# Graph attention on one core: three more tiles of the output pairs turned by VectorE, and another share of attention work beside the units ahead of the output stage

## The chip, the cores and the metric

The kernel runs on one core of a Trainium2 chip. The metric is the device time of one execution in microseconds (us). Before the change three runs gave 636.95, 638.43 and 638.96 us, so the median is 638.43 us.

The engines are named as in the profile: PE is TensorE (matrix products and transposes by a matrix product), PEld its weight loads, DVE is VectorE, ACT is ScalarE, POOL is GpSimd (here it mostly starts indirect gathers and scatters), SP is SyncE (here it only starts DMAs). "PEq", "ACTq", "SPq" are the sequencers of these engines.

## The reference

One layer of graph attention on 2708 nodes of 1024 features, in fp32, with a residual. `adj` is a random 0/1 matrix with some four ones in a row.

```python
h = relu(layernorm(x))                      # x: 2708 x 1024
q = h @ W_q.T + b_q;  k = h @ W_k.T + b_k;  v = h @ W_v.T + b_v
z = (q @ k.T) / sqrt(1024) * adj
z = where(z == 0, -10000, z)
out = x + relu(softmax(z, axis=1) @ v)
```

## The kernel before

Only the scores of existing edges are needed. The kernel sorts the nodes by their number of edges and cuts them into 21 full tiles of 128 nodes and a rest. Since z = h M h^T with M = scale * W_q^T W_k (plus a bias), PE forms M once, then q' = h M for the tiles; a score is the dot product of a row of q' with a gathered row of h. The weighted sum of rows of h is taken before W_v: u = sum(weight * h[neighbour]), and then out = relu(u W_v^T + b_v) + x.

**Units on PE.** PE multiplies two tiles at a time by Strassen's scheme (Winograd's form): a pair is a 256 x 1024 matrix in four blocks (a11 and a12 from the first tile, a21 and a22 from the second), and takes seven products instead of eight, each 8 records of 128x128 by 128x512 in the trace, about 3.43 us. The units are numbered: 0 to 9 are "q" pairs (tiles (0,1) to (18,19)), 10 to 19 are output pairs in the order (6,5), (4,3), (2,0), (20,7), (17,13), (18,12), (19,11), (15,10), (14,1), (16,9), and tile 8 alone stands behind them. So "the sixth output pair" is unit 15 with tiles 18 and 12, and the seventh is unit 16 with tiles 19 and 11. The operands are sums and differences of blocks: s1 = a22 + a21, s3 = a11 - a21, s2 = s1 - a11, s4 = a12 - s2 (L722, L742), and four sums and differences of W_v's blocks (T0 to T3, L1270, each 128x2048 elements), which VectorE forms in units 9 and 10, before the first output pair. After a unit's last product c22 (`q` L1092) and c12 (L1095) add PSUM banks on VectorE; PE's next product into the same bank waits for that.

**Turning a tile.** The operand must lie transposed. There are two ways.
- By PE: u is stored to `u_dram` by SP (L951) and loaded by SP as one DMA of 512 KB (L1212), or kept in SBUF (`held`) when its unit comes soon. PE transposes it in eight products of 128x128 (L415) into PSUM banks `pt`, ScalarE copies a11, a12 and a22 to SBUF (L718), and VectorE takes a21 from PSUM directly when it forms s1 and s3.
- "Faced": ScalarE copies u into another order of columns (v, L945) and stores it from its own queue (L947); SP loads it as four DMAs of 128 KB, each of 32 partitions (L700), so that four blocks of the 128x128 transpose already stand in their places; VectorE transposes 32x32 blocks within them (L705), one instruction of 128x512 for each of a11, a12, a22 and a21 (which stands in the buffer of s3). PE and the copies L718 are not needed.

**Attention as a stream.** The attention work is one generator, `attention`, of steps on VectorE. A score step is one multiply-and-accumulate with a gathered row tile (`junk` L863), a sum step adds one weighted row tile (`u` L923); a step is planned at 1.3 us. Between them stand small instructions for the softmax (L906 to L911), ScalarE's exponential (`w` L872) and ScalarE's first term of u (L912, or L889 for the tile numbered 21). Every tile gathered needs one of 11 buffers (g0 to g10, later also pieces of M's space), which its last reader frees.

**What sets the order.** After the fourth unit the order on VectorE is the one in which the program is written. After each product of a unit `advance(share)` lets the stream go on until its planned cost has reached `share` us, so a larger share puts more score and sum steps ahead of what the unit itself needs (blocks, c12, c22, differences). The orders of PE, ScalarE, POOL and SP come from a scheduler, so they shift when VectorE's program shifts. When tile t's sum is finished at `now` = [unit, place], where places 0 to 6 count the products, the condition at L940 decides whether it is faced. The share (L1238) goes down by 2.3/7 us a product for each faced tile of the next unit.

Lines for the steps below: L415, L718, L722, L742, L705 (turning), L700, L947, L951, L1212 (DMAs of u), L863, L923 (stream), L872, L889, L912 (ScalarE within the stream), L1100 (ScalarE's copy of c21), L760 (biases into PSUM banks), L1223 and L1224 (PE's sum of all rows of h and its copy), L1270 (W_v's sums), L1092 (c22), L1011 (products).

Of the kernel before, what the change touches and what calls it, by code (L numbers as in the profile page):

```python
# [65 lines left out]
def tile_preln_masked_attention(  # L66
# [144 lines left out]
    def row_tile(name):  # L211
        return work.tile([P, D], FT, tag="row", name=name, bufs=ROWS)
# [626 lines left out]
    def fill():  # L839
        while wanted and free:  # L840
            t, s = wanted.pop(0)
            g = free.pop(0)
            if s == K[t]:
                half = slice(HOSTS.index(t) * HP, (HOSTS.index(t) + 1) * HP)
                nc.gpsimd.dma_start(g[:HP], v_dram[half, :])
            else:
                with tc.issue_after(first_q[0].ins) if first_q else nullcontext():
                    gathered.append(gather(g, h_dram[:, :], t, s, P, skip=True))
            g_of[t].append(g)

    def chained(step):

        with tc.issue_after(chain[-1].ins):
            chain.append(step())
# [64 lines left out]
    def sums(t):  # L919
        u, coef, m = us.pop(t)  # L920
        for s in range(0 if t in EMPTY else 1, K[t]):
            fill()
            chained(lambda: nc.vector.scalar_tensor_tensor(  # L923
                u, g_of[t][s], coef[:, s:s + 1], u, op0=ALU.mult, op1=ALU.add))
            free.append(g_of[t][s])
            yield 1.3
        fill()
        if t in HOSTS:
            chained(lambda: nc.vector.scalar_tensor_tensor(
                u[:HP], g_of[t][K[t]][:HP], m[:HP, 3:4], u[:HP], op0=ALU.mult, op1=ALU.add))  # L930
            free.append(g_of[t][K[t]])
            yield 1.3
            fill()
        g_of.pop(t)
        if t == SECOND:
            nc.sync.dma_start(v_dram, u)
            whole_second.append(True)
            return
        unit = next((n for n, pair in enumerate(units) if pair[0] == "o" and t in pair[1:]), len(units))
        if now < [unit - 2, 2] and unit <= len(q_pairs) + 4 or unit >= len(units) - 1:  # L940
            faced_tiles.add(t)
        print("done", t, "at", now, "unit", unit, t in faced_tiles)
        if t in faced_tiles:
            v = row_tile(f"v_{t}")
            nc.scalar.copy(v.rearrange("p (a c r) -> p c a r", a=QUADS, r=QP),  # L945
                           u.rearrange("p (c a r) -> p c a r", a=QUADS, r=QP))
            nc.scalar.dma_start(u_dram[t * P:(t + 1) * P, :], v)  # L947
        elif near(t):
            held[t] = u
        else:  # L950
            nc.sync.dma_start(u_dram[t * P:(t + 1) * P, :], u)  # L951
        done.add(t)
# [7 lines left out]
    def attention(order):  # L960
        for t in order[:2]:
            ask(t)
        free.extend(slots)

        fetch(order[0])
        fill()
        yield 0.0
        marked(0, EARLY)
        yield 0.0
        after = order[1:] + [None, None]  # L970
        yield from scores(order[0], after[0])
        for i, t in enumerate(order):
            nxt = after[i]
            ahead = nxt is not None and K[t] + K[nxt] <= HIGH + 1
            part = scores(nxt, after[i + 1]) if nxt is not None else iter(())
            if ahead:

                for _ in range(min(2, K[nxt] - 1)):
                    yield next(part, 0.0)
            weights(t)  # L980
            yield 0.6
            if ahead:
                yield from part
            yield from sums(t)
            yield from part
# [8 lines left out]
    spent, now = [0.0], [0, 0]  # L994

    def near(t):

        return t == alone or any(t in unit[1:] for unit in units[:now[0] + 3] if unit[0] == "o")
# [193 lines left out]
    q_pairs = [(t, t + 1) for t in range(0, BARE, 2)]  # L1192
    o_pairs = [(order[i], order[i + 1]) for i in range(0, FULL - 1, 2)]
    alone = order[-1]
    units = [("q",) + p for p in q_pairs] + [("o",) + p for p in o_pairs]
# [20 lines left out]
    last_q = len(q_pairs) - 1  # L1216
# [13 lines left out]
    for n, unit in enumerate(units):  # L1230
# [4 lines left out]
            ordered.enter_context(tc.manual_schedule(engines={mybir.EngineType.DVE}))  # L1235
            nc.sync.dma_start(bp_dram, bp_sb[0:1, :])
        turn = n in (0, FIRST - 1)
        share = (20.9 if n < len(units) - 5 else 21.5) / 7  # L1238
        nxt = units[n + 1] if n + 1 < len(units) else None
        if nxt is not None and nxt[0] == "o":  # L1240
            share -= 2.3 / 7 * len(set(nxt[1:]) & faced_tiles)
# [321 lines left out]
```

## Time and profile before

| What | us |
|---|---|
| median of three runs | 638.43 |
| the profiled execution | 638.0 |
| its span | 636.3 |
| granted TensorE clock (share of full) | 0.995 |
| PE busy in the span | 624.6 |
| DVE busy | 525.7 |
| ACT busy | 283.5 |
| POOL busy | 361.8 |

All the times in what follows are counted from the start of the span. The stages are: M's formation until about 105, units 0 to 9 until about 365 (with the next unit's first two products drawn ahead), units 10 to 19 until about 610, the single tile until 627.3, and then the last additions and scatters. An instruction's row in the timeline has its start, its length, its engine, line, operation and tile; consecutive instructions of VectorE overlap by some 0.05 to 0.1 us, so that two in a row take a little less than the sum of their lengths. In brackets stand the idle time ahead of it and what ended this.

### The profile page before, as it was taken

Reading aid. Unit: us, or ns where it says so; the run is one execution under the profiler, and the core shown is the slowest. Engines: PE = TensorE matmul, PEld = TensorE weight load, DVE = VectorE, ACT = ScalarE, POOL = GpSimd, SP = SyncE. Lnnn points to the kernel's source line nnn. Section 1 sums busy time; section 2 is a strip of 40 time slices with the busy share of each in tenths; the row PEclk is TensorE's granted clock in tenths of the full one; section 3 lists DMA queues with packets and bytes.
Section 4 is the critical chain, followed back from the end, with each engine's and each line's share of the span. In section 5 each row is a group of like instructions: output and inputs, shape, how many; then the busy total and the mean of one; then the engine's idle time right before and its main releaser. Section 6 shows DMA issues by size and latency. Waiting matters only on the chain.

```text
span 636.3 us, 6139 instructions
## 1 busy us (share of the span) xinstructions
PE 624.6 (98%) x1627; PEld 315.5 (50%) x1627; DVE 525.7 (83%) x1021; ACT 283.5 (45%) x421; POOL 361.8 (57%) x383
## 2 busy tenths in 40 slices
PE   9999999999999999999999999999999999999994
PEld 5777766444444544444444434444444444444441
DVE  5999889897995755997889999999999989898341
ACT  3539975859667533424341243443343333422300
POOL 2649960975868277563742563576566777632431
PEclk9999999999999999999999999999999999999997
DMA  8998897598696439986699998999999999893761
GB/s 339 407 372 310 334 351 298 199 342 328 246 382 221 170 113 334 326 299 196 194 289 323 297 412 216 311 318 324 351 378 321 334 299 295 242 289 95 210 217 40
DMA packets 62352, 180.11 MB, mean 283 GB/s; under 512 B 10039, under 2 KB 17031, under 8 KB 61672
## 3 DMA queue, kind: packets, MB, share of 16 engines
q0 software_dynamic: 25136, 78.41, 39.4%
q1 hardware_dynamic: 31242, 80.19, 35.8%
q10 hardware_dynamic: 5934, 21.06, 8.5%
q8 instruction: 15, 0.25, 0.2%
q14 instruction: 25, 0.20, 0.1%
HBM read 147.23 MB, written 42.31 MB: 298 GB/s over the span
## 4 chain that ended last, share of the span: by engine, by line
PE 85%; DVE 6%; issue 4%; DMA 3%; SPq 1%; POOL 0%; ACT 0%; POOLq 0%; DVEq 0%; ACTq 0%
PE ps L1011 38%; PE psy L1011 28%; PE ps_y L476 6%; PE ps_x L476 4%; PE ps_z L476 4%; PE pt L415 3%; DVE u L923 2%; DMA g<-h_dram,tab 1%; DMA or<-u_dram 1%; DVE junk L863 1%; DVE s L722 1%; DVE wlow L1270 1%; PE ps_y L511 1%; SPq L700 1%; DVE q L1092 0%
## 5 line engine op out<-in xcount | busy, mean ns | idle before, releaser
L610 POOL DMA_INDIRECT g<-h_dram,tab x94 | 121.4, 1291 | 84.4 <-DVE u L923 31.1
L1011 PE MATMUL ps<-M,a 128*128 128x512 f32 x320 | 144.0, 593 | 0.0
L1011 PE MATMUL psy<-wlow,s 128*128 128x512 f32 x320 | 143.9, 592 | 0.0
L863 DVE SCALAR_TENSOR_TENSOR junk<-g,pq 128x1024 uint8<-128x1024 f32 x93 | 113.7, 1222 | 14.0 <-DMA g<-h_dram,tab 10.9
L1011 PEld LDWEIGHTS ps<-M,a 128*128 128x128 f32 x320 | 59.8, 190 | 70.8 <-issue 70.6
L1011 PEld LDWEIGHTS psy<-wlow,s 128*128 128x128 f32 x320 | 59.7, 190 | 70.2 <-issue 69.4
L923 DVE SCALAR_TENSOR_TENSOR u<-g,coef,u 128x1024 f32<-128x1024 f32 x69 | 88.4, 1281 | 6.9 <-ACT u L912 5.8
L389 DVE FIND_INDEX8 at<-ones,adj 128x8 uint32<-128x685 f32 (+1 forms) x88 | 74.5, 865 | 0.0
L1011 PE MATMUL psy<-wlow,a 128*128 128x512 f32 x160 | 72.0, 593 | 1.4 <-DVE q L1092 1.4
L1011 PE MATMUL ps<-M,s 128*128 128x512 f32 x160 | 72.1, 592 | 0.0
L1011 PE MATMUL ps<-wlow,s 128*128 128x512 f32 x160 | 72.0, 593 | 0.1
L368 ACT ACTIVATE sized<-adj 128x2708 uint8<-128x2708 f32 (+1 forms) x22 | 54.3, 2468 | 7.5 <-DMA adj<-in_adj_dram 6.2
L298 POOL TENSOR_TENSOR hsum<-hsum,x 128x256 f32<-128x256 f32 (+1 forms) x56 | 38.7, 729 | 25.6 <-DVE wlow L444 21.2
L1110 POOL DMA_INDIRECT y<-in_x_dram,tab x19 | 34.8, 1832 | 29.1 <-ACT y L1127 15.9
L1011 PEld LDWEIGHTS psy<-wlow,a 128*128 128x128 f32 x160 | 30.3, 190 | 40.0 <-issue 37.1
L1011 PEld LDWEIGHTS ps<-wlow,s 128*128 128x128 f32 x160 | 30.3, 190 | 38.6 <-issue 37.9
L1011 PEld LDWEIGHTS ps<-M,s 128*128 128x128 f32 x160 | 30.3, 190 | 38.1 <-issue 37.4
L912 ACT ACTIVATE u<-g,coef 128x1024 f32<-128x1024 f32 x18 | 20.7, 1147 | 32.1 <-DVE coef L911 32.1
L808 POOL DMA_INDIRECT out_dram<-y,tab x21 | 25.0, 1188 | 16.4 <-DVE flag L1354 6.1
L626 POOL DMA_INDIRECT tab_dram<-tab,pos_i x22 | 21.9, 995 | 20.7 <-DVE pos_i L689 15.3
L276 ACT ACTIVATE x<-x,r 128x1024 f32<-128x1024 f32 (+1 forms) x22 | 25.9, 1235 | 7.3 <-POOL r L266 7.3
L760 ACT COPY ps<-bp_sb 128x512 f32<-128x512 f32 x42 | 24.5, 595 | 7.2 <-DVE y L1145 6.7
(251 smaller groups left out, 843.5 us busy)
## 6 DMA issues: line engine op xcount, KB each, us to landing
adj<-in_adj_dram SPq DMA_DIRECT2D x21, 1354.0 KB, 11.3
x<-in_x_dram SPq DMA_DIRECT2D x21, 512.0 KB, 3.9
h_dram<-x ACTq DMA_DIRECT2D x21, 512.0 KB, 8.7
u_dram<-v ACTq DMA_DIRECT2D x13, 512.0 KB, 6.4
or<-u_dram SPq DMA_DIRECT2D x52, 128.0 KB, 7.0
q_late<-q SPq DMA_DIRECT2D x12, 512.0 KB, 6.0
pq<-q_late SPq DMA_DIRECT2D x12, 512.0 KB, 8.6
M<-in_wv_dram SPq DMA_DIRECT2D x4, 1024.0 KB
```

Of the source, the lines that this page charges most:

```text
L276: nc.scalar.activation(xs[i][:n], xs[i][:n], AF.Relu, bias=r[:n, 4, i:i + 1], scale=r[:n, 3, i:i + 1])
L298: small.append(nc.gpsimd.tensor_add(hsum[:n, cols], hsum[:n, cols], xt[:n, cols]))
L368: nc.scalar.activation(sized[:n], a[:n, :, :PW], AF.Abs, accum_out=total[:n, t:t + 1])
L389: nc.vector.max_index(at[:n, k - first_k, g, :], ones[:n, 0:8], a[:n, g, :])
L476: mm = nc.tensor.matmul(bank, a_tile(o + H * a[0], a[1], i), b(o), start=first and o == 0, stop=(o == H - 1), skip_group_check=True)
L610: return nc.gpsimd.indirect_dma_start(out=dst, out_offset=None, in_=src, in_offset=off, bounds_check=N - 1, oob_is_err=False)
L760: nc.scalar.copy(return_[h], row[:, h * NB:(h + 1) * NB])
L808: to = nc.gpsimd.indirect_dma_start(out=out, out_offset=bass.IndirectOffsetOnAxis(ap=ptab.bitcast(U32)[:n, t, SLOTS:SLOTS + 1], axis=0), i ...
L863: chained(lambda: nc.vector.scalar_tensor_tensor(junk, g_of[t][s], 1.0, tq[t], op0=ALU.mult, op1=ALU.mult, accum_out=zall[:, t, s:s + 1]))
L923: chained(lambda: nc.vector.scalar_tensor_tensor(u, g_of[t][s], coef[:, s:s + 1], u, op0=ALU.mult, op1=ALU.add))
L1011: mm = nc.tensor.matmul(bank, a[:, c, :], b[:, c, :], start=False, stop=(c == 3), skip_group_check=True)
L1110: return nc.gpsimd.indirect_dma_start(out=y[:n], out_offset=None, in_=x, in_offset=off, compute_op=ALU.add)
```

## The change

Two lines are changed. The first sets which tiles are faced: the condition now reaches to unit 16 instead of unit 14, and a tile must be finished before place 1, not place 2, of the unit two ahead of its own. The second sets the share of the stream: 21.6/7 us a product up to unit 7 (the stream starts in unit 5), 19.9/7 in units 8, 9 and 10, and 20.9/7 and 21.5/7 as before in the later units.

```diff
@@ L940
-        if now < [unit - 2, 2] and unit <= len(q_pairs) + 4 or unit >= len(units) - 1:
+        if now < [unit - 2, 1] and unit <= len(q_pairs) + 6 or unit >= len(units) - 1:
             faced_tiles.add(t)
@@ L1238
-        share = (20.9 if n < len(units) - 5 else 21.5) / 7
+        share = (21.6 if n < last_q - 1 else 19.9 if n < last_q + 2 else 20.9 if n < len(units) - 5 else 21.5) / 7
         nxt = units[n + 1] if n + 1 < len(units) else None
         if nxt is not None and nxt[0] == "o":
             share -= 2.3 / 7 * len(set(nxt[1:]) & faced_tiles)
```

Tiles 18, 12 and 19 are faced now, tile 11 is not. PE has 24 transposes fewer. VectorE has six more L705 (a11, a12, a22 and a21 of unit 15, a11 and a12 of unit 16). ScalarE loses five copies L718 and gets three copies L945 and three stores L947. SP loses four stores L951 and four loads L1212, and gets twelve loads L700: tile 15 of unit 17 is finished at place 0 of unit 15 instead of place 5 of unit 14, so that it is kept in SBUF and neither stored nor loaded. Units 14 and 15 have 4.6 and 2.3 us less of the stream beside them, since their next units have two faced tiles and one. Everything behind them in the stream comes that much later in the program.

PE, around the end of unit 14. `psy<-wlow,a22` is unit 14's last product, `s2` the first of unit 15's own. Before:

```order
L1011 MATMUL ps1_2910<-wlow_171,s1_2876 128x512 x4
L1011 MATMUL psy_2825<-wlow_171,a22_2740 128x512 x4
L415 MATMUL pt_2991<-ident_75,or_18_2928 128x128 x4
L415 MATMUL pt_2998<-ident_75,or_18_2928 128x128 x4
L1011 MATMUL psy_2950<-wlow_171,s2_2879 128x512 x4
L415 MATMUL pt_3027<-ident_75,or_12_2930 128x128 x4
L415 MATMUL pt_3034<-ident_75,or_12_2930 128x128 x4
L1011 MATMUL ps0_2908<-M_148,a12_2856 128x512 x4
```

Now:

```order
L1011 MATMUL ps1_2911<-wlow_171,s1_2878 128x512 x4
L1011 MATMUL psy_2826<-wlow_171,a22_2737 128x512 x4
L1011 MATMUL psy_2960<-wlow_171,s2_2881 128x512 x4
L1011 MATMUL ps0_2909<-M_148,a12_2851 128x512 x4
L1011 MATMUL ps1_2911<-M_148,s4_2883 128x512 x4
```

The four rows of transposes of tiles 18 and 12 are gone; those of tile 19 go in the same way one unit later.

VectorE at the same place: the last sum steps of tile 11, the score steps of tile 10, the weights of tile 15, and the blocks of unit 15. Before:

```order
L923 TENSOR_SCALAR u_11_2923<-g4_1407,coef_2922,u_11_2923 128x1024
L923 TENSOR_SCALAR u_11_2923<-M_148,coef_2922,u_11_2923 128x1024 x2
L863 TENSOR_SCALAR junk2_3008,zall_102<-g10_1413,pq_10_2963 128x1024
L863 TENSOR_SCALAR junk2_3010,zall_102<-g0_1403,pq_10_2963 128x1024
L906 TENSOR_SCALAR w_15_2977,m_15_3018<-w_15_2977,keys_93 128x4
L910 RECIPROCAL m_15_3018<-m_15_3018 128x1
L911 TENSOR_SCALAR coef_3019<-w_15_2977,m_15_3018 128x4
L863 TENSOR_SCALAR junk2_3025,zall_102<-g1_1404,pq_10_2963 128x1024
L722 TENSOR_TENSOR s1_3039<-a22_3032,pt_3034 128x512
L722 TENSOR_TENSOR s3_3041<-a11_2996,pt_3034 128x512
```

Now:

```order
L923 TENSOR_SCALAR u_11_2949<-g4_1407,coef_2948,u_11_2949 128x1024
L705 STREAM_TRANSPOSE a11_3002<-or_18_2927 128x4x4x32
L705 STREAM_TRANSPOSE a12_3004<-or_18_2927 128x4x4x32
L923 TENSOR_SCALAR u_11_2949<-M_148,coef_2948,u_11_2949 128x1024 x2
L863 TENSOR_SCALAR junk2_3016,zall_102<-g10_1413,pq_10_2975 128x1024
L863 TENSOR_SCALAR junk2_3018,zall_102<-g0_1403,pq_10_2975 128x1024
L705 STREAM_TRANSPOSE a22_3020<-or_12_2932 128x4x4x32
L705 STREAM_TRANSPOSE s3_3022<-or_12_2932 128x4x4x32
L722 TENSOR_TENSOR s1_3024<-a22_3020,s3_3022 128x512
L742 TENSOR_TENSOR s3_3022<-a11_3002,s3_3022 128x512
```

On SP's queue the loads for it, with `tail_dram<-y_20`, a store which waits for an output of unit 13. Before:

```order
L951 DMA u_dram_66<-u_19_2847 128x1024
L1130 DMA tail_dram_72<-y_20_2841 1x1024
L1212 DMA or_18_2928<-u_dram_66 128x1024
L1212 DMA or_12_2930<-u_dram_66 128x1024
L833 DMA pq_14_3071<-q_late_65 128x1024
```

Now:

```order
L700 DMA or_18_2927<-u_dram_66 32x4x256
L1130 DMA tail_dram_72<-y_20_2845 1x1024
L700 DMA or_18_2927<-u_dram_66 32x4x256 x3
L700 DMA or_12_2932<-u_dram_66 32x4x256 x4
L833 DMA pq_14_3097<-q_late_65 128x1024
```

Four transposes of VectorE stand among the stream's steps, and the first two wait for three loads that stand behind the store of y_20.

ScalarE around unit 8 (blocks of unit 9, `w_21` the exponential that needs the last of seven score steps, `u_21` the first term of that tile's sum). Before:

```order
L1027 COPY p5_2103<-ps1_2064 128x512
L1100 COPY q_15_1970<-psy_1938 128x512
L718 COPY a11_2127<-pt_2122 128x512
L718 COPY a12_2134<-pt_2129 128x512
L872 ACTIVATE w_21_2160<-zall_102 128x7
L760 COPY ps0_2216<-bp_sb_90 128x512
L889 ACTIVATE u_21_2164<-g0_1403,w_21_2160 128x1024
```

Now:

```order
L1027 COPY p5_2105<-ps1_2068 128x512
L872 ACTIVATE w_21_2154<-zall_102 128x7
L1100 COPY q_15_1972<-psy_1946 128x512
L718 COPY a11_2129<-pt_2124 128x512
L718 COPY a12_2136<-pt_2131 128x512
L889 ACTIVATE u_21_2158<-g0_1403,w_21_2154 128x1024
L760 COPY ps0_2217<-bp_sb_90 128x512
```

The exponential moved ahead of three copies that had been ready long before it.

## The prediction

> **What bounds the kernel now.** I read the page's table of busy times first, then who waited on PE, then the chain of waits, and after these VectorE's waits by stretch and the timelines at the places that the change touches. A row of the waits gives the engine and line that waited, whom for, us in total, times, and the longest.
>
> ```profile
> span 636.3 us, 6139 instructions
> PE 624.6 (98%) x1627; PEld 315.5 (50%) x1627; DVE 525.7 (83%) x1021; ACT 283.5 (45%) x421; POOL 361.8 (57%) x383
> PE psy L1011 <- DVE q L1092: 1.4, 1, 1.4
> ```
>
> PE is busy for 98% of the span. Within the units it waits once, 1.4 us for a c22 of VectorE. So work taken from PE shortens the run as long as the others keep up. The chain shows where this wait stands and what follows (start, length, what):
>
> ```profile
> 368.16 0.61 DVE q L1092
> 368.81 7.13 PE psy L1011 x16
> ...
> 389.74 3.67 PE ps L1011 x8
> ...
> 468.94 0.87 PE pt L415 x8
> ...
> 473.25 0.87 PE pt L415 x8
> ...
> 494.73 0.87 PE pt L415 x8
> ...
> 627.28 0.70 DVE y_alone L1379
> ```
>
> From 368.81 to 627.28 the chain is PE alone. Ahead of 368.81 it runs through VectorE. At 389.74 PE takes s1 of unit 11, which VectorE delivers only just in time (the row at 388.90, under the rivals). So a delay of VectorE up to there is a delay of PE, and only later is VectorE ahead. VectorE has almost no room in that long stretch (windows: us, then busy time and count of each engine, granted clock, DMA share, GB/s):
>
> ```profile
> 411.00:512.00 101.00, 101.00 (x261) 46.47 (x260) 95.51 (x155) 36.18 (x62) 67.22 (x51) 1.00 1.03 340
> ```
>
> It is busy for 95.5 of 101 us, and the DMA engines are full (share 1.03). The change puts work on both.
>
> **The change: PE's part.** Three groups of eight transposes go, those of tiles 18 and 12 (468.94, 473.25) and of tile 19 (494.73). Each is 0.87 us on the chain with PE before and behind it: 3 x 0.87 = 2.61 us. Nothing else is removed from PE or added to it, since tile 11 still goes through L415, and tile 15 too, only from another source. The five ScalarE copies L718 that go are beside PE at ACT's 45% and give PE nothing.
>
> **The run-up to 368.81.** By the new order, the same sum and score steps stand ahead of q_19's c22 as before; the larger share of units 5 to 7 is taken back by unit 8's smaller one. So the work ahead of that wait is the same, and only waits within it can move. What moves is on ScalarE:
>
> ```profile
> 306.23 0.23 DVE L911 TENSOR_SCALAR coef<-w,m 128x6 f32<-128x6 f32 x1
> ...
> 305.94 1.04 ACT L945 COPY v<-u 128x1024 f32<-128x1024 f32 x1 [3.18 <-DVE u L923]
> 306.89 1.14 ACT L912 ACTIVATE u<-g,coef 128x1024 f32<-128x1024 f32 x1
> ...
> 319.83 1.07 ACT L718 COPY a<-pt 128x512 f32<-128x512 f32 x2
> 324.42 0.21 ACT L872 ACTIVATE w<-zall 128x7 f32<-128x7 f32 x1 [3.51 <-DVE junk L863]
> 324.53 0.58 ACT L760 COPY ps<-bp_sb 128x512 f32<-128x512 f32 x1
> 325.04 1.14 ACT L889 ACTIVATE u<-g,w 128x1024 f32<-128x1024 f32 x1
> ...
> 324.32 1.88 PE L1223 MATMUL ps_h<-hsum,ones 128*128 128x512 f32 x4
> ...
> 326.22 2.61 DVE L923 SCALAR_TENSOR_TENSOR u<-g,w,u 128x1024 f32<-128x1024 f32 x2 [1.36 <-ACT u L889]
> ...
> 348.81 0.17 DVE L906 SCALAR_TENSOR_TENSOR w<-w,keys 128x8 f32<-128x8 f32 x1 [0.28 <-ACT w L872]
> ```
>
> The exponential L872 waits for a score until 324.42. Now L1100 and the two L718 stand behind it, ready or not. L889 then starts not 0.62 us after L872 but 0.11 + 0.5 (from a copy's start to the next's, as from L760 to L889) + 0.97 (the two L718, less their overlap) = 1.58 us after it, so VectorE's sum step at 326.22 is 0.95 us later. Two waits shrink against this. The u L912 at 306.89 began when the copy v ahead of it was done; the sum that v needs now ends one sum step sooner, ahead of a unit's blocks, so L912 starts when its weights are ready (L911 ends at 306.46), about 0.43 us sooner. The 0.28 us at 348.81 is covered by two transposes that now stand between the last score and this step. Net: +0.95 - 0.43 - 0.28 = +0.24 us on q_19, and by the zero slack at 389.7 also on PE's stream. Bounds: -0.7 (the two shrink, and L889 costs nothing, as the score comes earlier by as much) and +1.1 (neither of the two shrinks, and the third difference of W_v, which is moved about 2 us forward, waits a little for its block; no view gives that load's landing).
>
> PE gets a new wait ahead of it: the two products L1223 go into the PSUM banks that the two L718 free (four banks `pt` take turns), the first now at 324.42 + 0.60 + 0.58 = 325.6 instead of 320.9, so PE stands there for up to 1.3 us, some 0.85 with the 0.43. That costs nothing, as PE would otherwise wait 1.41 us at 368.81: the wait is moved, and what is left there is about 1.41 + 0.24 - 0.85 = 0.8.
>
> **VectorE behind it.** These are its waits between 386 and 592, and the rows of one turned tile:
>
> ```profile
> DVE u L923 <- ACT u L912: 2.8, 2, 1.6
> DVE junk L863 <- DMA M<-h_dram,tab: 1.8, 1, 1.8
> DVE junk L863 <- DMA g<-h_dram,tab: 1.8, 2, 1.0
> DVE p L1122 <- ACT taken L1076: 1.2, 2, 1.0
> DVE s L722 <- ACT a L718: 1.0, 1, 1.0
> 447.23 1.30 DVE L705 STREAM_TRANSPOSE a<-or 128x512 f32<-128x512 f32 x2
> 464.45 3.92 DVE L923 SCALAR_TENSOR_TENSOR u<-g,coef,u 128x1024 f32<-128x1024 f32 x3
> ```
>
> Six more transposes cost 6 x 0.65 = 3.9 us. The 1.0 us for L718 goes with the copies. Of the 3.6 us for gathered rows I let 3.0 go, since VectorE comes later to most of them, and all 1.2 us of `taken`, which PE paces. A new wait comes at the first two transposes. The place of the last sum step ends at 468.37 before; by the new order VectorE has one or one and a half steps less to do by then (at 1.3 us), so it gets there at about 467. The loads:
>
> ```profile
> 430.49 7.86 SPq L700 DMA_DIRECT2D or<-u_dram  x8
> 460.53 0.25 SPq L1130 DMA_DIRECT2D tail_dram<-y  x1
> 460.85 0.80 SPq L1212 DMA_DIRECT2D or<-u_dram  x2
> L700 SPq DMA_DIRECT2D or<-u_dram x52: 302/430/802, 325.5 to 599.1; - x52
> DMA to landing us min/median/max: 3.1/7.0/15.1
> 452.68 0.71 DVE L705 STREAM_TRANSPOSE a<-or 128x512 f32<-128x512 f32 x1 [0.49 <-DMA or<-u_dram]
> ```
>
> Three of tile 18's four loads are queued on SP behind the store L1130, which waits for its y until 460.53. At 0.43 us an issue (L700's median) the last of them is issued at 462.1 and lands, by the median, at 469.1: a wait of 2.1 us, between 0 and 10 with the least and the most of L700. The three stores that leave SP give its queue some 0.3 us each, which nothing waits for. So tile 8's sum, the last of the stream, is later by 0.24 + 3.9 - 1.0 - 3.0 - 1.2 + 2.1 = 1.0 us. The s1 of units 15 to 18 come later as well, but PE shows no wait at all for them now. The place where it can tell is the end:
>
> ```profile
> 591.14 1.27 DVE L929 SCALAR_TENSOR_TENSOR u<-g,m,u 64x1024 f32<-64x1024 f32 x1
> 605.03 1.25 DVE L705 STREAM_TRANSPOSE T_alone<-or 128x1024 f32<-128x1024 f32 x1 [11.56 <-DMA or<-u_dram]
> 609.69 3.60 PE L1011 MATMUL ps<-M,T_alone 128*128 128x512 f32 x8
> ```
>
> Tile 8's sum ends at 592.41, its turned copy at 606.28, and PE takes it at 609.69: 3.41 us of slack. PE comes 2.61 - 0.24 = 2.4 us earlier, so 1.0 is left, just what the 1.0 us above needs. I take 0 here, with 0 to 2.1 as bounds (2.1 in the first rival).
>
> **The sum.** 638.0 - 2.61 + 0.24 + 0 = 635.6 against the profiled execution, whose time lies 0.43 us under the median of the three runs, 638.43. Against that median: 636.0.
>
> Eight transposes of a tile cost PE 0.87 us and the two instructions that replace them cost VectorE 1.30. The Trainium skill, "VectorE: DVE Perf Modes", section Rules for kernel authors, says: "Transpose 128×128: Use TensorE if PSUM dest is OK". By that rule the change goes the wrong way, and the trace agrees in so far as VectorE is the slower one for a tile; by the chain PE is still the one that counts until VectorE's slack at the end is used up. The next paragraph works that out.
>
> **Rivals.** *VectorE's end becomes the bound.* If no gather wait and no `taken` goes and the loads are in time, tile 8 is later by 0.24 + 3.9 - 1.0 = 3.1, 2.1 beyond the slack: 638.0 - 2.4 + 2.1 = 637.7, or 638.1 by the median, no change. For it speaks the 95.5 of 101 us; against it that the gathers and `taken` come no later than before, while VectorE does.
>
> *The run-up costs more.* With +1.1 instead of +0.24 the sum is 636.5, or 636.9 by the median; within 0.3%. It hangs on the row of s1 of unit 11 (the sum that ends the run-up):
>
> ```profile
> 388.90 0.69 DVE L722 TENSOR_TENSOR s<-a,s 128x512 f32<-128x512 f32 x1
> ```
>
> It ends at 389.59, 0.1 us ahead of PE, which is why nothing hides such a delay.
>
> *The loads are late, and it is slower.* Twelve loads of 128 KB replace three of 512 KB while the DMA engines are full. The eight from 430.49 were all issued by 438.35, and the last landed only just ahead of 452.68, 14 us later. At 15.1 us tile 18's last load lands at 477.2: a wait of 10.2 instead of 2.1, tile 8's sum 8.1 us later still, and 638.0 - 2.4 + 8.1 = 643.7, or 644.1 by the median. It decides from 4.3 us beyond the slack (2.4 gained and 1.9, which is 0.3%), that is from a landing at about 473.4, 11 us after issue. Against it: the median is 7.0, and two loads fewer for tile 15 come just behind. The Trainium skill, "DMA: Bandwidth & Descriptors", section Bandwidth, advises batches of at least 1 MiB, and so speaks against the four parts; of 512 KB in one or in four, no view here shows the same place twice.
>
> **How the numbers follow.** About 0.3%, 1.9 us, is what a measurement of this kernel can tell from no change. My forecast, faster by more than that, gets 0.50, since the 2.61 us are sure and the two terms against them small in the middle. The first rival gets 0.20 and the second 0.12 (both no change). The third gets 0.16, slower. For 0.02 nothing here accounts; I put it to no change. So: faster 0.50, same 0.34, slower 0.16. The range goes from 634.1 (2.61 and 0.7 gained, 635.1 by the median, and 1.0 for the three runs, which lie 2.0 us apart) to 640.4, where the third rival starts.
>
> **What would show it.** In the changed profile: no L415 for tiles 18, 12 and 19; a wait of PE at L1223 of about 0.8 us and a smaller one at L1011 for L1092; the L718 wait of VectorE gone and one at L705 for `or` of about 2 us in its place; T_alone's transpose ending within 1 us of PE's product of it. The forecast is wrong if PE waits for T_alone, for s1 of units 15 to 18, or for more than 1.6 us in all around L1223 and L1092.

## The result and the profile after

The changed kernel takes 643.08 us (median of 22 runs, 636.53 to 649.16) against 638.18 us for the kernel before (22 runs on the same chip, 636.95 to 640.85). The ratio is 1.0072, with a 95% interval from 1.006 to 1.0084: slower by 0.7%, where the prediction had 0.4% faster. All ratios, here and below, leave out the executions that took over 1.5% longer than the fastest of the same kernel: here two of the changed kernel's 22 (647.36 and 649.16 us), below four of 12 in e2, five of 12 in e3 and two of 12 in e10. The profiled execution of the changed kernel took 643.1 us, close to its median, and its span is 641.3 us, 5.0 us longer than that of before.

The page's busy times and the waits of PE, after:

```profile
span 641.3 us, 6110 instructions
PE 624.4 (97%) x1603; PEld 313.5 (49%) x1603; DVE 529.6 (83%) x1027; ACT 284.0 (44%) x419; POOL 354.6 (55%) x383
...
PE ps L1011 <- DVE T_alone L705: 3.1, 1, 3.1
PE ps L1011 <- DVE s L722: 2.0, 2, 1.3
PE psy L1011 <- DVE q L1092: 1.6, 1, 1.6
```

PE's records fall from 1627 to 1603, the 24 transposes. In their place come two kinds of waits within the units that the kernel before did not have: for tile 8's turned copy, and for s1 of units 11 (0.65) and 19 (1.32). PE's timeline at the end, and the granted clock (the column behind POOL's busy time) in the windows around T_alone, first before, then after:

```profile
613.00:618.00 5.00, 5.00 (x14) 2.31 (x13) 0.76 (x2) 0.59 (x1) 0.28 (x1) 1.00 0.09 37
```

```profile
589.01 3.67 PE L1011 MATMUL ps<-wlow,s 128*128 128x512 f32 x8 [1.32 <-DVE s L722]
...
612.92 5.40 PE L1011 MATMUL ps<-M,T_alone 128*128 128x512 f32 x8 [3.08 <-DVE T_alone L705]
618.15 3.60 PE L1011 MATMUL psy<-wlow,a 128*128 128x512 f32 x8
...
613.00:618.00 5.00, 5.00 (x8) 2.12 (x9) 4.69 (x9) 0.59 (x1) 2.84 (x3) 0.66 0.91 310
```

PE stands 3.08 us ahead of T_alone, and then half of the product runs at half the clock: from 612.92 to 618.15 are 5.23 us instead of 3.43. So the account is: -2.61 (transposes) + 0.22 (longer wait at q_19) + 0.65 + 1.32 + 3.08 + 1.80 (half clock) + 0.23 (PE is that much later already at 319, 319.37 against 319.14, ahead of the places that the prediction speaks of) = 4.69. The other 0.3 of the 5.0 us is small pieces, most of it at the two last waits: PE loses 1.50 and 3.24 us there, as the rows count a wait from the modelled end of the product ahead of it.

Why T_alone is late, is read from VectorE's rows, from its waits between 386 and 596, and from the chain that ended last:

```profile
597.13 1.27 DVE L929 SCALAR_TENSOR_TENSOR u<-g,m,u 64x1024 f32<-64x1024 f32 x1
...
611.62 1.25 DVE L705 STREAM_TRANSPOSE T_alone<-or 128x1024 f32<-128x1024 f32 x1 [12.15 <-DMA or<-u_dram]
```

```profile
DVE u L923 <- ACT u L912: 4.2, 3, 1.6
DVE junk L863 <- DMA g<-h_dram,tab: 3.3, 3, 2.0
DVE a L705 <- DMA or<-u_dram: 2.5, 2, 1.9
```

```profile
498.33 3.45 PE ps L1011 x8
507.55 7.41 DMA g<-h_dram,tab
518.80 8.87 DMA g<-h_dram,tab
599.51 4.38 DMA u_dram<-v
605.33 6.26 DMA or<-u_dram
```

Tile 8's sum ends at 598.40, 6.0 us later than before (592.41). The waits for L718 and for `taken` have gone, and one for `or` has come, as forecast. But the waits for gathered rows, 3.6 us before, are still 3.3, and those for L912 grew from 2.8 to 4.2. The chain, which from 368.81 on was PE alone, now runs through two gathers. Gathers are issued by GpSimd, in order, and GpSimd's queue has changed. Its rows, before and then after:

```profile
481.11 2.17 POOL L1110 DMA_INDIRECT y<-in_x_dram,tab  x1 [0.30 <-issue]
...
490.63 0.91 POOL L808 DMA_INDIRECT out_dram<-y,tab  x1 [2.81 <-DMA y<-in_x_dram,tab]
491.85 1.29 POOL L808 DMA_INDIRECT out_dram<-y,tab  x1 [0.30 <-issue]
493.45 1.04 POOL L610 DMA_INDIRECT g<-h_dram,tab  x1 [0.30 <-DMA pq<-q_dram,tab]
```

```profile
488.43 1.42 POOL L1110 DMA_INDIRECT y<-in_x_dram,tab  x1 [0.30 <-DMA out_dram<-y,tab]
490.15 1.65 POOL L808 DMA_INDIRECT out_dram<-y,tab  x1 [0.30 <-issue]
492.11 1.01 POOL L612 DMA_INDIRECT pq<-q_dram,tab  x1 [0.31 <-issue]
498.44 1.03 POOL L808 DMA_INDIRECT out_dram<-y,tab  x1 [5.31 <-DMA y<-in_x_dram,tab]
499.77 1.09 POOL L610 DMA_INDIRECT g<-h_dram,tab  x1 [0.30 <-issue]
```

L808 at 498.44 is the scatter of y_21, the rest tile. Its gather-add L1110 is issued at 488.43 and lands 9 us later; GpSimd stands 5.31 us there, and the next gather for the stream is issued at 499.77 instead of 493.45. From then on GpSimd issues back to back, some 1.3 us each, and cannot catch up. Before, y_21's gather-add was the one at 481.11 and took 9 us to land as well, but it was issued 7.3 us sooner, and its scatter at 490.63 had to wait only 2.81 us. So the stand comes from GpSimd's new order, in which the gather-add stands further back. Its load L1183, to which it adds, also leaves later: on SP it stands behind eight of the new quarter loads, until 471.78 (464.93 before). That this late load is what moved the gather-add back is not shown, since in the row at 488.43 GpSimd does not wait for it.

The run-up has waits of its own. VectorE's waits between 262 and 392, before and then after:

```profile
DVE junk L863 <- DMA g<-h_dram,tab: 4.0, 2, 3.1
DVE u L923 <- ACT u L912: 3.0, 2, 1.6
DVE u L923 <- ACT u L889: 1.4, 1, 1.4
...
DVE s L722 <- ACT a L718: 0.2, 1, 0.2
```

```profile
DVE u L923 <- ACT u L912: 2.4, 2, 1.2
DVE u L923 <- ACT u L889: 2.3, 1, 2.3
DVE junk L863 <- DMA g<-h_dram,tab: 2.2, 1, 2.2
DVE s L722 <- ACT a L718: 1.7, 1, 1.7
DVE wlow L1270 <- DMA M<-in_wv_dram: 1.7, 2, 1.1
```

L889 costs 0.9 us more and L912 0.6 less, much as worked out. Two waits are new: 1.7 us for a copy L718, and 1.7 us at the differences of W_v. The first is ScalarE's order again, one unit earlier than where the prediction looked:

```profile
273.94 0.23 DVE L911 TENSOR_SCALAR coef<-w,m 128x4 f32<-128x4 f32 x1
275.86 1.28 DVE L722 TENSOR_TENSOR s<-a,pt 128x512 f32<-128x512 f32 x2 [1.69 <-ACT a L718]
...
274.20 1.15 ACT L912 ACTIVATE u<-g,coef 128x1024 f32<-128x1024 f32 x1 [0.94 <-DVE coef L911]
275.26 0.57 ACT L718 COPY a<-pt 128x512 f32<-128x512 f32 x1
```

L912 waits for weights that VectorE finishes at 274.17. The copy of a22 behind it could have run at 273.3, when L1055 was done and its transposes too. VectorE needs this copy next, and so waits for 1.69 us. Before, the copy stood ahead of L912 and ran at 273.12. In this execution the gather waits of the stretch went down from 4.0 to 2.2, which made up for much of it.

### The profile page after: what moved, and what is told of

Read it like the earlier page. It is cut to its first block, busy times and chain, and to the rows that moved or that the text cites. A ratio compares the mean times of both kernels' runs of the same rounds, so it can differ in the third digit from the quotient of the medians.

```text
span 641.3 us, 6110 instructions
## 1 busy us (share of the span) xinstructions
PE 624.4 (97%) x1603; PEld 313.5 (49%) x1603; DVE 529.6 (83%) x1027; ACT 284.0 (44%) x419; POOL 354.6 (55%) x383
## 4 chain that ended last, share of the span: by engine, by line
PE 73%; DVE 12%; DMA 7%; issue 4%; POOL 1%; ACT 1%; SPq 0%; POOLq 0%; DVEq 0%; ACTq 0%
PE ps L1011 32%; PE psy L1011 22%; PE ps_y L476 6%; DVE u L923 4%; PE ps_z L476 4%; PE ps_x L476 4%; PE pt L415 3%; DMA g<-h_dram,tab 3%; DVE junk L863 2%; DMA or<-u_dram 2%; DMA u_dram<-v 2%; DVE s L722 1%; DMA M<-in_wv_dram 1%; DVE a L705 1%; PE ps_y L511 1%
## 5 line engine op out<-in xcount | busy, mean ns | idle before, releaser
L610 POOL DMA_INDIRECT g<-h_dram,tab x94 | 111.4, 1185 | 86.5 <-DVE u L923 35.1
L1110 POOL DMA_INDIRECT y<-in_x_dram,tab x19 | 34.6, 1822 | 37.3 <-ACT y L1127 24.7
L808 POOL DMA_INDIRECT out_dram<-y,tab x21 | 28.3, 1346 | 17.4 <-DMA y<-in_x_dram,tab 7.4
L912 ACT ACTIVATE u<-g,coef 128x1024 f32<-128x1024 f32 x18 | 20.7, 1148 | 30.4 <-DVE coef L911 20.2
L945 ACT COPY v<-u 128x1024 f32<-128x1024 f32 x16 | 16.7, 1045 | 30.5 <-DVE u L923 22.0
```

The lines of the kernel that those rows point to most:

```text
L610: return nc.gpsimd.indirect_dma_start(out=dst, out_offset=None, in_=src, in_offset=off, bounds_check=N - 1, oob_is_err=False)
L808: to = nc.gpsimd.indirect_dma_start(out=out, out_offset=bass.IndirectOffsetOnAxis(ap=ptab.bitcast(U32)[:n, t, SLOTS:SLOTS + 1], axis=0), i ...
L1110: return nc.gpsimd.indirect_dma_start(out=y[:n], out_offset=None, in_=x, in_offset=off, compute_op=ALU.add)
```

## The experiments

All ratios are to the kernel before, measured beside each experiment on the same chip, with 95% intervals. The kernel before had medians of 640.1 to 642.0 us on these other chips, and there PE also waited 1.4 to 2.5 us for a gathered row (`qr`) at about 203 in the profile of each experiment, so microseconds of different chips are not compared. The change itself was not measured again on them.

### The two lines of the change, each alone

```diff
e1:  share = (21.6 if n < last_q - 1 else 19.9 if n < last_q + 2 else ...) / 7    (condition as before)
e2:  if now < [unit - 2, 1] and unit <= len(q_pairs) + 6 or unit >= len(units) - 1:    (share as before)
```

> The old condition for faced tiles, the new share alone. Theory E (the end): the loss of the change stands at the last tile, whose sum VectorE finishes too late because of six more transposes; the new share alone costs only what the trace of the change shows at 369 and 391 us, 0.2 + 0.65 us of PE waits: about 639.1 us, with no wait of PE for T_alone. Rival S (the share): the order of the stream is what makes VectorE late, through new waits at 324 to 391 us and behind them: 641.5 us or more, with a wait for T_alone of at least 1.5 us.

> The new condition for faced tiles, the old share. Theory E: still slow, about 642.2 us (the 643.1 of the whole change less 0.9), PE waits about 2 to 3 us for T_alone, and the two waits at 369 and 391 us are as in the kernel before (1.4 and 0). Rival S: the 2.6 us of transposes are gained in full, 635.6 us, with no wait for T_alone.

e1: 1.0053 (1.0024 to 1.0082). e2: 1.0065 (1.0032 to 1.0098). Each line alone makes the kernel slower, so there are two causes: theory E fits the time of e2, theory S that of e1, and neither fits both. The two costs added, 1.2%, are more than the 0.7% of the change; whether they overlap or the chips differ, no run tells. The new share, with no tile more faced, costs some 3.4 us. PE's waits in its profile:

```profile
PE psy L1011 <- DVE q L1092: 3.2, 1, 3.2
```

The wait at q_19 is 3.2 us, and PE also waits 0.6 us at L1223; at T_alone there is none. The profiled execution of e2 took 638.29 us, well under its median of 645.7, and shows only 1.5 us at T_alone; it doesn't explain the median.

### Is it tile 8's way to PE?

Tile 8 is kept in SBUF and turned by PE at place 1 of the last unit, with the change (e3) and with the new condition alone (e4), so that nobody waits for its store and loads.

```diff
-        if ... or unit >= len(units) - 1:
+        if ... or unit == len(units) - 1:
-                faces(uT, single["rows"], 0, DC)
+                for s in range(NH):
+                    nc.scalar.copy(uT[:, s * 4:s * 4 + 4, :], half_turned(single["rows"], s))
```

> The whole change, and the last tile 8 is kept in SBUF and turned by PE (eight transposes, two copies of ScalarE) instead of by store, four loads and VectorE. That takes some 13 us out of the chain from tile 8's sum to PE. Theory E: the 3.1 us wait for T_alone and the 2.0 us of slower products behind it go, 0.9 us of transposes come: 643.1 - 5.1 + 0.9 = 638.9 us. Rival S: nothing of the loss is at the end, so 0.9 us slower than the change: 644.0 us.

> The new condition with the old share, and tile 8 turned by PE as in the run before. Theory E: 2.6 us of transposes gained, 0.9 given for tile 8, no wait for T_alone, perhaps 1.3 us at s1 of the last pair: 636.5 to 637.8 us. Rival S: 636.5 us, and the run with the old share and tile 8 turned by VectorE is faster than this by 0.9.

1.006 (1.0021 to 1.0099) and 1.0071 (1.0044 to 1.0098). e4 is slower than either expectation had. In e3 PE's transposes themselves wait 2.4 us for tile 8's sum, and the two waits of the run-up are there (2.4 at q_19, 0.9 at L1223). The place was too early, so e3 doesn't show that the way through memory is harmless. It shows that the sum is late, whichever way it is turned.

### Is it VectorE's own time?

e5 is the kernel before with six unused steps of 128x512 on VectorE at the places of the six new transposes. e6 is the change without the last two sum steps of tiles 10 and 14 (its output lacks them). e7 and e8 let GpSimd form s4 of units 14 to 19, in the change and with the condition alone.

```diff
e5: +  junk = work.tile([P, D], mybir.dt.uint8, tag="junk", ...)
    +  nc.vector.scalar_tensor_tensor(junk[:, :NB], hsum[:, :NB], 1.0, hsum[:, NB:], op0=ALU.mult, op1=ALU.mult)   (six in all)
e6: +  if t in (10, 14) and s >= K[t] - 2:
    +      free.append(g_of[t][s])
    +      continue
e7, e8: -  put("s4", ops["a12"], ops["s2"], ALU.subtract, eng)
        +  put("s4", ops["a12"], ops["s2"], ALU.subtract, nc.gpsimd)   (units 14 to 19; shortened)
```

> The kernel before, with six more VectorE instructions (128x512, about 0.65 us each, their result is not used) at the places where the change turns its three tiles; no tile more is faced, no DMA and nothing of PE is changed. Theory V (VectorE's own time): the 3.9 us go through to the last tile almost in full, because VectorE's waits move along with it; tile 8's sum is 3 to 5 us later, PE, whose slack there is 3.4 us, waits up to 1.5 us for T_alone: ratio to before 1.000 to 1.003, and T_alone's slack of 3.4 us is gone in the profile. Rival D (the small loads): without the twelve loads VectorE takes the six steps into its waits; tile 8's sum is at most 1 us later, T_alone keeps 2.4 us of slack or more, ratio 1.000.

> The whole change, and four sum steps (128x1024, 1.3 us each) are left out: the last two of tile 10 and of tile 14, so that their rows lack two neighbours. The loads and the copies of the change stay. Theory V: with 5.1 us less on VectorE the waits of PE for T_alone (3.1 us, and 1.7 us of slow products behind it) and for s1 of the last pair (1.3 us) go: 6.1 us less than the change, 637.0 us on the scale of the first runs, ratio to before 0.998. Rival D: the loads remain late, tile 8's sum is at most 1 us earlier, ratio 1.005 to 1.007.

> The whole change, and the difference s4 of units 14 to 19 is formed by GpSimd instead of VectorE (six instructions of 0.63 us less on VectorE, 3.8 us). Theory V: as far as in the run before, nearly: no wait for T_alone or one under 0.5 us: 638 us on the scale of the first runs, ratio 0.998 to 1.001. Rival D: ratio 1.005 to 1.007. If GpSimd's gathers come late behind the differences, VectorE waits for them instead, and the ratio is 1.007 or more.

> The new condition with the old share, s4 of units 14 to 19 on GpSimd. Theory V: the 2.6 us of transposes are gained and the run-up is as before: 635.6 to 637 us on the scale of the first runs, ratio 0.996 to 0.999. Rival D: as with the new condition alone, ratio 1.005 or more.

e5: 1.0005 (0.9991 to 1.0019): the six steps cost nothing. In its profile no wait for a gathered row is left between 386 and 592, which is just what the prediction had let go. e6: 1.0104 (1.008 to 1.0128), with 5 us less to do on VectorE: slower than either expectation had. Its gather waits grew to 8.7 us, and GpSimd stands at the same scatter:

```profile
500.44 1.80 POOL L808 DMA_INDIRECT out_dram<-y,tab  x1 [5.82 <-DMA y<-in_x_dram,tab]
```

e7: 1.0132 (1.0098 to 1.0166), e8: 1.009 (1.0074 to 1.0106): with this work on GpSimd e7 is slower than the change, and e8 lies above e2, though within the intervals. So VectorE's additional 3.9 us are not the cause by themselves. That points to what feeds VectorE, and here to GpSimd.

### GpSimd's stand at the rest tile

The scatter of y_21 is put further on, behind the gather-add of y_18: with the change (e9), with the condition alone (e10), and in the kernel before as a control (e11). e12 makes the stand without the change: the kernel before, with y_21's load one place later.

```diff
e9, e10, e11:
-        sent.insert(0, (y, t, n))
+        rest.append((y, t, n))
             sent.append((y, t, P))
+            if t == 13:
+                sent.append(rest.pop())
e12:
-            if i == 3 and units[n - 1][0] == "o" and NT - 2 in units[n - 1][1:]:
+            if i == 4 and units[n - 1][0] == "o" and NT - 2 in units[n - 1][1:]:
```

> The change, with the scatter of the rest tile y_21 (L808) taken out of its place behind pq_1 on GpSimd's queue and put some 20 rows further on, behind the gather-add of y_18; nothing is left out. Theory G (GpSimd stands 5.3 us at that scatter, and the gathers behind it come late to VectorE): the wait at L808 for y_21 is under 1 us, VectorE's waits for gathered rows between 386 and 592 fall from 3.3 to under 1.5 us, tile 8's sum ends at 594 to 596 instead of 598.4, PE's wait for T_alone is under 1 us, and the time is 0.997 to 1.003 of before. If GpSimd's stand has nothing to do with it (the loads of the faced tiles, ScalarE's order, VectorE's own work), the time stays at 1.005 or more, with the waits of PE at the end as they were.

> The new condition with the old share, and the scatter of y_21 put further on in the same way. Theory G: 0.995 to 1.000 of before (the 2.6 us of transposes without the run-up's cost). Otherwise, as without the late scatter, 1.005 or more.

> Control: the kernel before with the scatter of y_21 put further on. Theory G: its wait of 2.8 us on GpSimd goes, VectorE's gather waits shrink a little, and since PE waits for neither the time is 0.998 to 1.001. A time clearly under 0.998 would say that the edit is good for something else than what it undoes in the change.

> The kernel before with the load of y_21 from tail_dram (L1183) one place later in the program, which puts it behind the load of tile 19 on SP's queue and leaves GpSimd's order as it is. Theory G: GpSimd's stand at y_21 grows from 2.8 us to 4 to 8, VectorE waits 2 to 4 us more for gathered rows, and the time goes up to 1.001 to 1.006 of before; the wait of PE for T_alone appears if tile 8's sum is late by over 3.4 us. If GpSimd's stand costs nothing, 1.000.

e9: 1.0039 (1.001 to 1.0069). e10: 1.0005 (0.9973 to 1.0037). e11: 1.002 (0.9991 to 1.0049). e12: 0.9991 (0.9967 to 1.0015). The edit does nothing for the kernel before that the measurement shows, takes 0.6% from the condition alone (1.0065 to 1.0005), and about 0.3% from the change (1.0072 to 1.0039, at the edge of the intervals), each on another chip. In e9 and e10 VectorE waits for no gathered row between 386 and 596 any more, and in e9's profile tile 8's sum ends 225.2 us after VectorE's c22 of q_19, in that of the change 229.2. Theory G holds as a part of the change's cost. e9 came out above what it had expected (1.0039 against at most 1.003, and 1.4 us for T_alone against under 1); the run-up is still there:

```profile
PE psy L1011 <- DVE q L1092: 2.2, 1, 2.2
...
PE ps L1011 <- DVE T_alone L705: 1.4, 1, 1.4
...
PE ps_h L1225 <- ACT a L718: 1.2, 1, 1.2
```

e12 was a miss for the theory as I had put it:

```profile
494.19 1.08 POOL L808 DMA_INDIRECT out_dram<-y,tab  x1 [5.50 <-DMA y<-in_x_dram,tab]
```

The stand is as long as in the change and costs nothing. Its tile 8 has room: the turned copy is ready at 610.4 and PE takes it at 612.70. So the stand alone uses up some 1.1 of the 3.4 us of slack, and no more. In the change the 2.6 us of transposes are gone from PE's way to tile 8, and most of this slack with them.

e10's profile shows something else, the loads of the faced tiles:

```profile
476.89 1.30 DVE L705 STREAM_TRANSPOSE a<-or 128x512 f32<-128x512 f32 x2 [6.46 <-DMA or<-u_dram]
484.20 0.71 DVE L705 STREAM_TRANSPOSE a<-or 128x512 f32<-128x512 f32 x1 [2.42 <-DMA or<-u_dram]
...
493.17 5.40 PE L1011 MATMUL psy<-wlow,a 128*128 128x512 f32 x8 [2.73 <-ACT taken L1076]
```

This is the third rival. The eight quarter loads stand on SP behind L1130 until 461.58, and the last of them lands at 484.18, 17 us after its issue. PE, which waits for nothing there in the profile of the change, stands 2.73 us at 493.17 for ScalarE's copy `taken`, which follows VectorE's late steps, and has half of the next product at half the clock. e4's profile shows the same: 8.8 us at L705, and 2.41 us of PE for `taken`. On the other hand no profile of the new condition alone has the long stand: the scatter of y_21 waits 2.8 us in e2's and 0.3 in e4's. So for the condition alone the gain by the late scatter rests on the measured times, and what the profiles show is the late loads.

### The two new waits of the run-up, the loads, and two additions together

e13 takes the first difference of W_v one place later, e14 does this and the late scatter. e15 has the new condition, the old share, the late scatter, and the store L1130 and the load L1183 on ScalarE's queue. e16 is the kernel before with the additions of e5 and e12 together.

```diff
e13, e14:
-            for at, place, a, b in (((0, 2), T[:, 0], b12, b11), ...
+            for at, place, a, b in (((0, 3), T[:, 0], b12, b11), ...
e15:
-                nc.sync.dma_start(tail_dram, ya[P - 1:, :])
+                nc.scalar.dma_start(tail_dram, ya[P - 1:, :])
-        nc.sync.dma_start(y[:n], tail_dram.to_broadcast([n, D]))
+        nc.scalar.dma_start(y[:n], tail_dram.to_broadcast([n, D]))
```

> The change, with VectorE's first difference of W_v's blocks (T0, L1270) taken at place 3 of unit 9 instead of place 2, so that some two steps of the stream stand ahead of it; nothing is left out. Theory R (in the run-up VectorE now reaches this difference before its load has landed, and waits 1.1 to 2.5 us, which goes on to q_19 and PE): no wait of VectorE at L1270 for M's load, PE's wait at q_19 1 to 2.5 us shorter, and 0.2 to 0.4% of the change's cost gone: 1.003 to 1.005 of before; the waits of PE for T_alone stay. If the run-up's cost comes from ScalarE's order alone, the time stays at 1.007.

> The change with both edits: T0 one place later and the scatter of y_21 further on. Theories R and G together: the late scatter alone came to 1.004, so 1.000 to 1.002. If neither adds to the other, 1.004.

> The new condition with the old share, the late scatter of y_21, and the store L1130 and the load L1183 of the rest tile on ScalarE's queue, so that tile 18's loads no longer stand behind L1130 on SP. Theory L (VectorE's waits for faced loads, 9.2 us in the profile without this edit, come from these loads being issued late and together): tile 18's loads are issued before 461, VectorE's waits at L705 between 386 and 592 fall under 3 us, PE waits for neither T_alone nor a c22, and the time is 0.995 to 0.999 of before. If the DMA engines set it (the loads land late however early they are issued), the waits stay above 5 us in sum and the time at 1.000 or more.

> The kernel before with both of two additions that cost nothing each by itself: six more VectorE steps of 128x512 at the places of the faces (3.9 us of work), and the load of y_21 one place later (GpSimd stands 5.5 us at its scatter). Theory G: the two don't add up linearly; with the gathers late VectorE's gather waits don't go, so that tile 8's sum ends 226 to 228.5 us after q_19's c22 (223.6 with the steps alone, 224.3 with the stand alone, 229.2 in the change), and PE waits up to 1.5 us for T_alone: 1.000 to 1.003. If VectorE's work is absorbed anyway, 223.5 to 224.5 and 1.000.

e13: 1.0135 (1.0084 to 1.0186), a clear miss. The first difference no longer waits and PE's wait at q_19 is 0.7 us, but the third difference, in the next unit, waits instead, and s1 of unit 11 behind it comes late:

```profile
382.02 2.29 DVE L1270 TENSOR_TENSOR wlow<-M 128x2048 f32<-128x2048 f32 x1 [2.83 <-DMA M<-in_wv_dram]
...
399.34 5.37 PE L1011 MATMUL ps<-wlow,s 128*128 128x512 f32 x8 [2.02 <-DVE s L722]
```

e14: 1.0082 (1.005 to 1.0114), a miss too (1.000 to 1.002 was expected). It is less than e13, which fits a late scatter that takes its part here too, but the intervals overlap. The wait for W_v can't be moved away like this.

e15: 1.0016 (0.9981 to 1.0051), above the 0.995 to 0.999 expected. VectorE's waits at L705 are 0.8 us, so in this profile the loads are in time once they don't stand behind L1130. PE still waits 1.2 us for T_alone. That is what the first rival said, though smaller: 2.6 us of transposes saved, 1.2 given back. In the median of 12 runs nothing of it is left, and why that is, the one profile (638.3 us of span, shorter than most) can't tell.

e16: 0.9981 (0.9952 to 1.001). It was to show that the stand and VectorE's additional work cost something together, but its profile has a stand of only 2.9 us, so it leaves this open.

### Which half of the new share?

```diff
e17:  share = (21.6 if n < last_q - 1 else 20.9 if n < len(units) - 5 else 21.5) / 7
e18:  share = (20.9 if n < last_q - 1 else 19.9 if n < last_q + 2 else 20.9 if n < len(units) - 5 else 21.5) / 7
```

> The kernel before with only the first half of the new share: 21.6/7 us a product up to unit 7, from unit 8 on as before. ScalarE's first term L912 stands ahead of the copy L718 of unit 7's a22 as in the change, so VectorE waits 1.7 us at L722 about 275; the difference of W_v comes two small groups later than in the change, so no wait at L1270. Some two steps (2.6 us) stand ahead of q_19's c22 in addition. Theory R1 (the wait at L722 and the work ahead set the cost of the share): PE waits 3 to 5 us at q_19, 1.004 to 1.008 of before. If the share's cost came from the wait for W_v alone, 1.000 to 1.002.

> The kernel before with only the second half of the new share: 19.9/7 us a product in units 8, 9 and 10. No wait at L722 about 275; VectorE comes about one or two steps earlier to the first difference of W_v and waits 2 to 4 us for its load, but stands no later at q_19 than before, because it has that much less to do ahead of it. Theory R1: PE's wait at q_19 as before (0 to 2 us), the stream's end up to 2.6 us later, within its slack of 3.4: 0.998 to 1.002. If the wait for W_v sets the share's cost, 1.003 to 1.006.

e17: 1.0181 (1.0146 to 1.0216). e18: 0.9997 (0.9976 to 1.0018). VectorE's waits from 262 to its c22 of q_19, first e17, then e18:

```profile
DVE u L923 <- ACT u L889: 2.3, 1, 2.3
DVE s L722 <- ACT a L718: 1.7, 1, 1.7
DVE u L923 <- ACT u L912: 1.2, 1, 1.2
DVE wlow L1270 <- DMA M<-in_wv_dram: 1.0, 1, 1.0
```

```profile
DVE u L923 <- ACT u L912: 2.8, 2, 1.6
DVE u L923 <- ACT u L889: 1.4, 1, 1.4
```

All three waits come with the larger share up to unit 7, the one for W_v's block too, which I had put to the other half; the smaller share of units 8 to 10 brings none of them and costs nothing that the measurement shows. e17 is slower than the change and than its expectation (1.004 to 1.008). Nothing takes the additional steps back there: PE also waits 3.3 us for s1 of unit 11, and VectorE 3.9 and then 7.4 us for a row of `pq` which is loaded from `q_late`, which neither expectation had. No version here beats the kernel before beyond its interval.

## Why the prediction was wrong

**PE's 2.61 us** were right: the 24 records are gone, and nothing else changed on PE.

**The run-up** (+0.24, bounds -0.7 to +1.1) was mis-sized. Its three sizes were right: L889 +0.95 (measured 2.30 against 1.36), the u L912 -0.43 (1.62 to 1.22), and the 0.28 gone. The step that failed is "What moves is on ScalarE", followed by a look at one place only. At 275 the same reordering puts a copy L718 behind L912, with 1.69 us; it was in the order of ScalarE one unit ahead of the place shown. And the wait for W_v's load, which I had inside the bound as "a little" and at the third difference, was 0.59 us there and 1.08 at the first (2.52 in e1's profile). The new share alone measured 0.53% or some 3.4 us, with 0.24 to 0.82% as its interval; in the profiled execution only 0.9 us of it shows (0.22 at q_19 and 0.65 at s1 of unit 11), as gather waits ahead of it shrank. The new wait at L1223 was right in kind: none in the profile of the change itself, 0.4 to 1.2 in e1, e3, e9, e13, e14 and e17. But it did not shorten the wait at q_19, which was 2.2 and 3.2 us in e9 and e1.

**VectorE behind it** is the step that failed most: "Of the 3.6 us for gathered rows I let 3.0 go, since VectorE comes later to most of them". VectorE does come later, but so do the gathers. With a late VectorE alone all of the 3.6 us go (e5); in the change 3.3 remain, as GpSimd stands 5.3 us at the scatter of y_21. I went along SP's queue only for tile 18's loads, not on to y_21's load behind eight quarter loads, and never to GpSimd's order, where y_21's gather-add had moved back. The other terms held: 1.0 for L718 and 1.2 for `taken` are gone, and L705 waits 2.5 us in all (2.1 and the former 0.5 forecast). A further 1.4 us at L912 was not foreseen. Tile 8's sum came 6.0 us later instead of 1.0.

**The end** (0, bounds 0 to 2.1) follows from it: 3.08 us for T_alone, 1.32 for s1 of unit 19, and 1.80 for the half clock, which no term had.

**The rivals.** The first, VectorE's end as the bound, happened in kind, but larger: tile 8's sum came 6.0 us later and not 3.1, as the waits at L705 (2.5) and the growth at L912 (1.4) were not in it. The second happened too: 0.9 us in the profile of the change, within its own +1.1, and 3.4 us by the measurement of the new share alone, beyond it. The third, late loads, shows in the profiles of e4 and e10 (8.8 and 9.2 us at L705, and PE waits of 2.41 and 2.73 us behind them) and not in that of the change (2.5), so it is a part in some executions. The Trainium skill's rule in "VectorE: DVE Perf Modes", section Rules for kernel authors (TensorE for a 128x128 transpose), pointed the right way in the result, but not for VectorE's time: e5 spends that time and measures no change.

**What stays open.** The new condition with both mends (e15) should gain 1.2 to 1.4 us by its profile, and measured none. That the stand costs in the change since the slack is gone, is argued from e12's slack and the 2.6 us taken from PE; e16, which was to try it, didn't have the stand. How much of the new condition's 0.65% is the stand and how much the late loads, the runs don't separate.

## What to carry to other kernels

Before putting a term "this wait goes, as the engine comes later", follow the queue that feeds the wait through every engine, as the same edit may delay the feeder; here one gather-add stood further back in GpSimd's order, its scatter waited for it, and all the gathers behind the scatter came late. Read the order of each in-order engine over the whole stretch where the program shifts, since an instruction that waits for its input takes all behind it along, and one such place found is no sign that it is the only one. When work leaves the engine that bounds the kernel, the slack of everything that it waits for shrinks by the same amount, so what cost nothing before has to be costed anew.

## What was not expected of the hardware

A short wait of PE can cost more than its length. In the 20 profiles of this study (before, after and the 18 experiments) there are 25 waits of PE of 2.0 to 3.3 us (from 130 us on); behind 14 of them some four of the following products start 0.85 us apart instead of 0.43, for some 3.4 us, which is 1.7 us lost (seven products in e8). Behind 28 waits of 1.3 to 2.0 us there is none. The row 613.00:618.00 above (clock 0.66 over 5 us) is one such place. The Trainium skill, "TensorE: Matmul & The Clock Gate", section What's actually happening, has the half clock "after ≥1 idle window (~3.4µs)", with windows that run freely. The length of the slow stretch agrees with such a window, the condition doesn't: 2.0 us idle were enough in three cases, and 3.3 us not in another.
